# Graph stack on one Trainium2 core: z of four batches turned by VectorE, five more rows through DRAM, row columns stored element by element

## The chip, the core and the metric

One core of one Trainium2 chip runs the whole program. It has five engines that run beside each other: TensorE (PE in the profile, with PEld for its weight loads), VectorE (DVE), ScalarE (ACT), GpSimd (POOL) and the queue engine SyncE (SP), which here only issues DMAs. The metric is the device time of one execution in microseconds; lower is better. The time before is the median of three runs.

## The reference

Four layers run one after the other on `x` of 16 batches x 1024 nodes x 256 features, all in float32, with one weighted adjacency `adj` (1024 x 1024, some 1.6% of it set, the diagonal included):

```python
# layer 0: edge scores, a masked sum, a plain sum
S   = sigmoid(relu(h@W1[:d] [u] + h@W1[d:] [v] + b1) @ W2 + b2)   # one per edge u, v
z   = beta1*h + beta2*((S*A).T @ h @ Wa + ba) + beta3*((A.T @ h)*h @ Wm + bm)
# layer 1
z   = z + relu(A @ z @ W.T + b)
# layers 2 and 3: attention over all nodes, with adj as a bias, each with its own weights
feats  = z @ W1.T
f1     = feats @ W2 + b2
coefs  = softmax(leaky_relu(f1[:, None] + f1[None, :]) + adj)
z      = coefs @ feats + bias2 + z
```

The change lies in layers 2 and 3 only. Layer 3's result, node by feature, is the output.

## The kernel before, in words

**Tiling.** A node tile is 128 nodes (`P`), so a batch has eight (`NT`); a half is 512 nodes (`HN`, two of them, `NV`, four tiles each, `HT`). Between layers z is kept feature-major: `z[i]` is 128 partitions x 2 feature halves (`DH`) x 1024 nodes. The 16 batches go in four groups of four (`GB`, `NGR`).

**The main stream.** After the score-free work of all batches, each group runs `with_edges` (the masked sum of layer 0), `layer_one` for two batches at a time, and then layers 2 and 3 of its batches. Groups 0 to 2 do this in `group_layers`, in the order layer 2 of batches 0 to 3, layer 3 of batches 0 to 3. The last group runs as two pairs in `pair_layers`. A layer of a batch is made of:

- `front`: eight node tiles, each two products with the weights, giving `f` (feats and, in column D, f1 without its constant). PE writes a bank, ACT copies it out (L1392).
- the scale of the softmax: the code needs f1 of all nodes along a row in every partition (`r`), and the largest of them. It has two ways. `scales` (when `row` is None) turns the eight columns of f and the column of maxima by nine PE transposes. `to_row` (when a DRAM row is given) turns one 128 x 9 column tile by a PE transpose, copies it out by ACT, stores it in DRAM with a queue of SP (L1415) and loads it back twice, spread over all partitions (`rho`, L1416, and `tops`, L1417); `from_row`, some ticks later, takes the maximum on DVE (L1422) and goes on with a Relu on ACT (L1424). Both end in `scaled`.
- `sums`: twice (v = 0, 1) eight steps jt; in each DVE builds a tile m of 128 x 512 (L1475) and PE multiplies it with f into four banks. Three m tiles are built ahead (`AHEAD`).
- `second` or `third`: the end of a half. `second` turns the result back to feature-major and adds it to z. `third` makes the output: it needs z node-major, so `early` adds the bias to z on ACT (L1896) and turns two node tiles at a time by PE into a bank at the steps jt = 6 and 7 (L1905); `finish` adds that bank on DVE (L1921) and stores to `out` from ACT's queue.

**Order.** `later` is a list of work with a count of ticks. `tick` is called in `front` (two times), in `sums` (at every even jt) and in `projected` of layer one; what falls due is written at that place. `front` of the next batch is written ahead of `sums` of the current one, so a row made by `to_row` has the whole of the current `sums` before it is used; that of a group's first front has the second `layer_one`. A side stream of edge scores for the next group (gathers and scatters by POOL, products on DVE, sums on ACT) is woven in by `side.along`, and in the last group a stream that gathers layer one's messages by lists (`with_lists`). The framework then orders each engine's instructions by its own estimate of times, so the order on an engine is not exactly the written one; `paced` holds an instruction behind a recent product.

**Buffers that the change touches.** Eight PSUM banks; `gd_pool` (four tiles for edge scores, in the last pair for `msg`); `zs` with tag `u` (two tiles of the side stream's sources); `row_d`, a DRAM row per layer and batch.

Of the kernel before, what the change touches and what calls it, by code (L numbers as in the profile page):

```python
# [81 lines left out]
def gnn_stack_kernel(  # L82
# [41 lines left out]
    def bank():  # L124
        return psum[-1].tile([P, HN], F32, tag="bank", name="bank")
# [70 lines left out]
    R = 1 + D  # L196
# [92 lines left out]
    NGR = B // GB  # L289
# [636 lines left out]
    with tc.If(listed > 0) as arm:  # L926
        with ExitStack() as stack:
# [452 lines left out]
            def front(x, weights, row=None):  # L1380

                doing[0] = "fronts"
                wT = weights.wT
                f = ttile("feats").rearrange("p (t d) -> p t d", t=NT)
                for jt in range(NT):
                    ps = bank()
                    for dh in range(DH):
                        product(
                            ps[:, : D + 1], x[:, dh, jt * P : (jt + 1) * P], wT[:, dh, :],
                            start=dh == 0, stop=dh == DH - 1,  # L1390
                        )
                    nc.scalar.activation(f[:, jt, :], ps[:, : D + 1], AF.Copy)  # L1392
                    if jt % 4 == 1:
                        tick()
                    yield 0.86
                made = {}
                if row is None:
                    top = small.tile([P, 1], F32, tag="top", name="top")
                    nc.vector.tensor_reduce(top, f[:, :, D], AX.X, ALU.max)
                    later.append([1, lambda: scales(f, weights, made, top)])  # L1400
                else:
                    column = small.tile([P, NT + 1], F32, tag="column", name="column")
                    nc.vector.tensor_copy(column[:, :NT], f[:, :, D])
                    nc.vector.tensor_reduce(column[:, NT:], f[:, :, D], AX.X, ALU.max)
                    later.append([2, lambda: to_row(f, weights, made, row, column)])
                return made

            def to_row(f, weights, made, row, column):

                r = two.tile([P, N], F32, tag="rho", name="rho")  # L1410
                tops = two.tile([P, P], F32, tag="tops", name="tops")
                ps = bank()
                nc.tensor.transpose(ps[: NT + 1, :P], column, ident)
                nc.scalar.activation(r[: NT + 1, :P], ps[: NT + 1, :P], AF.Copy)
                nc.sync.dma_start(row.rearrange("(t p) -> t p", p=P), r[: NT + 1, :P])  # L1415
                nc.sync.dma_start(r, bcast_rows(row[:N], N))  # L1416
                nc.sync.dma_start(tops, bcast_rows(row[N:], P))  # L1417
                later.append([4, lambda: from_row(f, weights, made, r, tops)])
# [42 lines left out]
            def sums(made, v, finish, early=None):  # L1461

                doing[0] = "sums"
                while "f" not in made:
                    tick()
                f, r, ta = made["f"], made["r"], made["ta"]
                ms = made.setdefault("m", [])
                steps = made.setdefault("steps", [(w, jt) for w in range(NV) for jt in range(NT)])
                acc = [bank() for _ in range(HT)]
                for jt in range(NT):  # L1470
                    while steps and len(ms) < AHEAD:
                        w, kt = steps.pop(0)
# [12 lines left out]
                    if jt % 2 == 0:  # L1485
                        tick()
                    if early:
                        early(v, jt)
                    yield 1.7
                finish(v, acc)  # L1490
                yield 1.2

            def with_adj(main):

# [392 lines left out]
                return finish  # L1887


            def third(z, i, b):  # L1890
                turned_back = []

                def early(v, jt):
                    if v == 0 and jt == 2:
                        for dh in range(DH):
                            nc.scalar.activation(  # L1896
                                z[i][:, dh, :], z[i][:, dh, :], AF.Identity, bias=gat3.bias2[:, dh : dh + 1]
                            )
                    if jt < NT - 2:
                        return  # L1900
                    ps = bank()
                    for k in range(2):
                        it = v * HT + (jt - NT + 2) * 2 + k
                        for dh in range(DH):
                            nc.tensor.transpose(  # L1905
                                ps[:, k * D + dh * P : k * D + (dh + 1) * P],
                                z[i][:, dh, it * P : (it + 1) * P], ident,
                            )
                    turned_back.append(ps)

                def finish(v, acc):
                    for c in range(0, HT, 2):
                        ps = turned_back.pop(0)
                        it = v * HT + c
                        st = four.tile([P, 2, D + 1], F32, tag="st", name="st")
                        share = small.tile([P, 2], F32, tag="share", name="share")
# [9 lines left out]
                        later.append([1, functools.partial(nc.scalar.dma_start, to, st[:, :, :D])])  # L1926
                return finish, early

            def pair_layers(b, z, first):

                yield from first

                m0 = yield from front(z[0], gat2)
                m1 = yield from front(z[1], gat2)
                yield from sums(m0, 0, second(z, 0))
                yield from sums(m0, 1, second(z, 0))
                yield from sums(m1, 0, second(z, 1))
                m0 = yield from front(z[0], gat3)
                yield from sums(m1, 1, second(z, 1))
                t0, t1 = third(z, 0, b), third(z, 1, b)  # L1940
                yield from sums(m0, 0, *t0)
                m1 = yield from front(z[1], gat3)
                yield from sums(m0, 1, *t0)
                yield from sums(m1, 0, *t1)
                yield from sums(m1, 1, *t1)
                catch_up()

            def group_layers(g, z):
# [1 line left out]

                made = {}

                def fronts(layer, i, row=True):
                    row = row_d[layer, g * GB + i] if row else None
                    made[layer, i] = yield from front(z[i], (gat2, gat3)[layer], row)

                def next_hw(hw, k):
                    hw.append(load_hw((g + 1) * GB + k))
# [6 lines left out]
                def spread(loads):  # L1965

                    for k, load in enumerate(loads):
                        later.append([1 + 3 * k // 2, load])

                order = [(layer, i) for layer in range(2) for i in range(GB)]  # L1970
                beside = (lambda main: main) if g else with_adj
                yield from beside(layer_one(z[:2]))
                yield from fronts(0, 0, row=False)
                yield from beside(layer_one(z[2:]))
                assert not to_load and not to_exp
                for n, (layer, i) in enumerate(order):
                    if n + 1 < len(order):
                        yield from fronts(*order[n + 1])
                    if n == 2 * GB - 2:
                        hw, nz = [], load_z(g + 1)  # L1980
                        spread([functools.partial(next_hw, hw, k) for k in range(GB - 1)] + [next_z] * 2)
                    if n == 2 * GB - 1:
                        spread([functools.partial(next_hw, hw, GB - 1), next_z])
                    ends = third(z, i, g * GB) if layer else (second(z, i),)
                    yield from sums(made[layer, i], 0, *ends)
                    if n == 2 * GB - 1:
                        soon(g + 1)
                    yield from sums(made[layer, i], 1, *ends)
# [32 lines left out]
            for g in range(NGR):  # L2021
# [6 lines left out]
                else:  # L2028
# [2 lines left out]
                    with_lists(itertools.chain(  # L2031
                        first_pair, pair_layers(g * GB, z[:2], layer_one(z[:2], wide_quarters))
                    ))
                    for _ in pair_layers(g * GB + 2, z[2:], from_lists(z[2:], msg)):
                        pass
            assert next(side.steps, "end") == "end"
            psum.pop()
# [130 lines left out]
```

## Time and profile before

| what | us |
|---|---|
| median of three runs | 2999.75 (2998.23 to 3000.82) |
| the profiled execution's own time | 2996.18 |
| its span, first to last instruction | 2994.5 |
| PE busy | 2969.8 |
| PEld, DVE, ACT, POOL busy | 2139.4, 2107.0, 1828.2, 1711.4 |
| granted TensorE clock | 1.000 throughout |

The layers' sums run in these stretches, by the time of L1403 and L1399 in the trace: group 0 from 1082 to 1431 us, group 1 from 1613, group 2 from 2141 to 2489, the first pair from 2690, the second from 2845 to the end. A line of the profile's list of groups gives a line of the kernel, engine, operation, output and inputs, shape and count; behind the first bar the busy time of the group and the mean duration of one in ns; behind the second the idle time of the engine just before, and what ended it. A line of the timeline gives the start and the length in us, engine, line, operation and count. SPq means the queue instructions of SP.

### The profile page before, as it was taken

The numbers are of one execution on the slowest core, as the hardware profiler recorded it, in microseconds if no ns is written. First come the engines' busy times: TensorE is split into PE (matmuls) and PEld (weight loads), VectorE is DVE, ScalarE is ACT, GpSimd is POOL, SyncE is SP. The second block draws the span as 40 slices with busy tenths as digits, with TensorE's granted clock in tenths as the row PEclk, the third lists the DMA queues.
The fourth block names the chain that finished last, engine by engine and source line by source line (L and its number), as shares of the span: only waits on it lengthen the run. The fifth ranks groups of instructions, "written<-read, shape, count | busy, mean of one in ns | idle before, by whom it ended". The sixth has DMA issues, their size and how long they took to land. (4 is left out here: it accounts for less than half of the span.)

```text
span 2994.5 us, 41906 instructions
## 1 busy us (share of the span) xinstructions
PE 2969.8 (99%) x11750; PEld 2139.4 (71%) x11750; DVE 2107.0 (70%) x4173; ACT 1828.2 (61%) x6522; POOL 1711.4 (57%) x1501
## 2 busy tenths in 40 slices
PE   8999999999999999999999999999999999999999
PEld 5545555555548757888875788888568888858888
DVE  8877666666775677888666888876678843388744
ACT  3436665666766776787776678777767833213342
POOL 1136576677664757766667767667677520277500
PEclk9999999999999999999999999999999999999999
DMA  8899999989999986668988766899876546586600
GB/s 292 316 385 313 317 320 285 299 239 276 272 313 349 313 301 193 173 191 293 329 285 268 218 181 186 283 348 292 272 208 176 158 143 210 170 295 180 168 1 30
DMA packets 323467, 736.78 MB, mean 246 GB/s; under 512 B 51533, under 2 KB 145802, under 8 KB 318106
## 3 DMA queue, kind: packets, MB, share of 16 engines
q0 software_dynamic: 129664, 394.14, 44.1%
q1 hardware_dynamic: 152170, 268.05, 26.6%
q10 hardware_dynamic: 41392, 71.84, 6.4%
q8 instruction: 95, 1.56, 0.2%
q14 instruction: 146, 1.20, 0.1%
HBM read 597.34 MB, written 136.53 MB: 245 GB/s over the span
## 5 line engine op out<-in xcount | busy, mean ns | idle before, releaser
L1034 ACT ACTIVATE z<-z 128x257 f32<-128x257 f32 x2432 | 984.3, 410 | 455.8 <-DVE z L1068 272.5
L143 PE MATMUL bank<-feats,m 128*128 128x257 f32 x4096 | 908.3, 380 | 3.3 <-DVE m L1475 2.2
L143 PEld LDWEIGHTS bank<-feats,m 128*128 128x128 f32 x4096 | 769.7, 190 | 112.9 <-DVE m L1475 2.6
L946 POOL DMA_INDIRECT z<-v_d,slot_v x512 | 596.2, 1164 | 379.7 <-ACT z L1034 180.4
L951 POOL DMA_INDIRECT dense_d<-gt,slot_at x512 | 578.1, 1129 | 212.5 <-PE bank L143 117.9
L1066 DVE TENSOR_TENSOR z<-z,u 128x580 f32<-128x580 f32 x608 | 462.1, 760 | 323.4 <-PE bank L143 254.0
L1034 ACT ACTIVATION_READ_ACCUMULATOR z<-z 128x1 f32 x2432 | 467.4, 192 | 0.0
L1475 DVE SCALAR_TENSOR_TENSOR m<-rho,tau,adj_sb 128x512 f32<-128x512 f32 x512 | 377.1, 747 | 111.7 <-PE bank L143 104.2
L143 PE MATMUL bank<-gc,hw 128*128 128x256 f32 x1920 | 416.8, 379 | 2.9 <-ACT gc L1517 2.3
L143 PEld LDWEIGHTS bank<-gc,hw 128*128 128x128 f32 x1920 | 363.9, 190 | 55.1 <-ACT gc L1517 4.3
L1067 DVE TENSOR_TENSOR z<-z,u 128x448 f32<-128x448 f32 x608 | 376.9, 620 | 0.0
L143 PE MATMUL bank<-w1p,hT 128*128 128x385 f32 x1024 | 340.6, 486 | 2.4 <-DVE sign L629 1.2
L143 PEld LDWEIGHTS bank<-w1p,hT 128*128 128x128 f32 x1024 | 192.9, 189 | 149.8 <-issue 19.9
L143 PE MATMUL bank<-g_wT,z 128*128 128x257 f32 x1024 | 230.4, 380 | 0.5 <-DVE z L1678 0.5
L143 PE MATMUL bank<-adj_sb,h 128*128 128x512 f32 x504 | 223.3, 592 | 0.8 <-ACT stage L257 0.8
L143 PEld LDWEIGHTS bank<-g_wT,z 128*128 128x128 f32 x1024 | 192.0, 190 | 31.1 <-issue 2.4
L374 ACT ACTIVATE st<-bank 128x385 f32<-128x385 f32 x256 | 122.9, 485 | 140.4 <-PE bank L143 108.1
L946 POOL DMA_INDIRECT z<-v_d,x_node x96 | 124.2, 1293 | 119.5 <-PE bank L143 55.3
L143 PEld LDWEIGHTS bank<-adj_sb,h 128*128 128x128 f32 x504 | 95.5, 190 | 115.6 <-issue 106.5
L1068 DVE TENSOR_TENSOR z<-z,sign 128x128 f32<-128x128 f32 x608 | 173.7, 286 | 0.0
L1517 ACT ACTIVATE gc<-gd 128x512 f32<-128x512 f32 x112 | 126.4, 1138 | 74.7 <-PE bank L143 47.3
L143 PE MATMUL bank<-adjT_in,t 128*128 128x512 f32 x336 | 147.6, 592 | 0.0
(257 smaller groups left out, 3327.1 us busy)
## 6 DMA issues: line engine op xcount, KB each, us to landing
gd<-dense_d SPq DMA_DIRECT2D x128, 512.0 KB
dense_d<-zero ACTq DMA_DIRECT2D x64, 512.0 KB
h<-in_x_dram SPq DMA_DIRECT2D x19, 1024.0 KB
adjT_in<-sumT_d SPq DMA_DIRECT2D x70, 256.0 KB
u_d<-st SPq DMA_DIRECT2D x128, 128.5 KB
v_d<-st SPq DMA_DIRECT2D x128, 128.5 KB
u<-u_d POOLq DMA_DIRECT2D x32, 514.0 KB
hw_d<-st SPq DMA_DIRECT2D x128, 128.0 KB
```

The source lines that it names most:

```text
L143: recent.append(nc.tensor.matmul(*args, **kw))
L374: nc.scalar.activation(st[:, cols], ps[:, :half], AF.Copy)
L946: return paced(nc.gpsimd.indirect_dma_start(out=dst, out_offset=None, in_=src[:], in_offset=bass.IndirectOffsetOnAxis(ap=at, axis=0), **how,))
L951: return paced(nc.gpsimd.indirect_dma_start(out=dst[:], out_offset=bass.IndirectOffsetOnAxis(ap=at, axis=0), in_=src, in_offset=None,))
L1034: nc.scalar.activation(zk[:, c, :], zk[:, c, :], AF.Copy, accum_out=s[:, k, c : c + 1])
L1066: paced(nc.vector.tensor_tensor(big, big, uk[:, :, :BIG], ALU.max))
L1067: paced(nc.vector.tensor_tensor(low, low, uk[:, :, BIG:], ALU.min))
L1068: nc.vector.tensor_tensor(mixed, mixed, sign[:, None, :].to_broadcast([P, GB, MIXED]), ALU.mult)
L1475: nc.vector.scalar_tensor_tensor(m, r[:, cols], ta[:, kt : kt + 1], ea[:, kt, cols], ALU.max, ALU.mult)
L1517: paced(nc.scalar.activation(t, scores, AF.Copy), 16 - 2 * i)
```

## The change

Three edits.

1. In group 2 (layer 3 of batches 2 and 3) and in the last pair (layer 3 of both), z is turned to node-major by DVE instead of PE. Right behind the `front` that reads z, ACT adds the bias, and 32 DVE transposes of 32 x 32 blocks are listed in `to_turn`, each over 32 partitions x 256 elements. `sums` takes two from the list at every step jt, so they lie beside the sixteen steps ahead of the batch's own layer 3. The result goes to borrowed SBUF tiles (`gd` tiles, for batch 3 of group 2 two `u` tiles); `early` does nothing for these batches and `finish` reads the tiles.
2. Five more fronts take the way over DRAM: the first front of groups 0 to 2, and layer 2 of the second batch of both pairs.
3. `to_row` stores the column tile (128 partitions x 9) directly, element by element, without PE and ACT, and it falls due one tick earlier.

```diff
@@ front
-                    later.append([2, lambda: to_row(f, weights, made, row, column)])
+                    later.append([1, lambda: to_row(f, weights, made, row, column)])
@@ to_row
-                ps = bank()
-                nc.tensor.transpose(ps[: NT + 1, :P], column, ident)
-                nc.scalar.activation(r[: NT + 1, :P], ps[: NT + 1, :P], AF.Copy)
-                nc.sync.dma_start(row.rearrange("(t p) -> t p", p=P), r[: NT + 1, :P])
+                nc.sync.dma_start(row.rearrange("(t p) -> p t", p=P), column)
@@ sums
                     if early:
                         early(v, jt)
+                    for _ in range(2):
+                        if to_turn:
+                            to_turn.pop(0)()
                     yield 1.7
...
+            to_turn = []
@@
+            def turned_by_vector(x, room):
+                for dh in range(DH):
+                    nc.scalar.activation(x[:, dh, :], x[:, dh, :], AF.Identity, bias=gat3.bias2[:, dh : dh + 1])
+                Q = 32
+                for v in range(NV):
+                    cols = slice(v * HN, (v + 1) * HN)
+                    src = x[:, :, cols].rearrange("p h (t c q) -> p h t c q", c=P // Q, q=Q)
+                    dst = room[v].rearrange("p (t h a r) -> p h t a r", h=DH, a=P // Q, r=Q)
+                    for a in range(P // Q):
+                        for c in range(P // Q):
+                            to_turn.append(functools.partial(
+                                nc.vector.transpose, out=dst[c * Q : (c + 1) * Q, :, :, a, :],
+                                in_=src[a * Q : (a + 1) * Q, :, :, c, :],
+                            ))
+                return room
@@ third
-            def third(z, i, b):
+            def third(z, i, b, nodes=None):
                 def early(v, jt):
+                    if nodes is not None:
+                        return
...
-                        ps = turned_back.pop(0)
+                        if nodes is None:
+                            ps = turned_back.pop(0)
+                        else:
+                            ps = nodes[v][:, c * D : (c + 2) * D]
@@ pair_layers
-                m1 = yield from front(z[1], gat2)
+                m1 = yield from front(z[1], gat2, row_d[0, b + 1])
...
                 m0 = yield from front(z[0], gat3)
+                n0 = turned_by_vector(z[0], gd_room()) if by_vector else None
                 yield from sums(m1, 1, second(z, 1))
-                t0, t1 = third(z, 0, b), third(z, 1, b)
+                t0 = third(z, 0, b, n0)
                 yield from sums(m0, 0, *t0)
                 m1 = yield from front(z[1], gat3)
+                n1 = turned_by_vector(z[1], gd_room()) if by_vector else None
+                t1 = third(z, 1, b, n1)
@@ group_layers
-                yield from fronts(0, 0, row=False)
+                yield from fronts(0, 0)
...
                         yield from fronts(*order[n + 1])
+                        if order[n + 1][0] and g == NGR - 2 and order[n + 1][1] > 1:
+                            at = order[n + 1][1]
+                            nodes[at] = turned_by_vector(z[at], gd_room() if at < GB - 1 else [
+                                zs.tile([P, GB * R], F32, tag="u", name="zn")[:, : HT * D] for _ in range(NV)
+                            ])
...
-                    ends = third(z, i, g * GB) if layer else (second(z, i),)
+                    ends = third(z, i, g * GB, nodes.get(i)) if layer else (second(z, i),)
@@ the last group
-                    for _ in pair_layers(g * GB + 2, z[2:], from_lists(z[2:], msg)):
+                    for _ in pair_layers(g * GB + 2, z[2:], from_lists(z[2:], msg), True):
```

More of the change, by code (lines that the diff above doesn't have):

```diff
@@ L1887, in second, with gd_room @@
                 return finish
-            def third(z, i, b):
+            def turned_by_vector(x, room):
[13 more added lines that the diff above has]
+                return room
+            def gd_room():
+                return [
+                    gd_pool.tile([P, QN, GB], F32, tag="gd", name="zn").rearrange("p a b -> p (a b)") for _ in range(NV)
+                ]
+            def third(z, i, b, nodes=None):
                 turned_back = []
                 def early(v, jt):
+                    if nodes is not None:
+                        return
                     if v == 0 and jt == 2:
@@ L1927, in third, with pair_layers @@
                 return finish, early
-            def pair_layers(b, z, first):
+            def pair_layers(b, z, first, by_vector=False):
                 yield from first
                 m0 = yield from front(z[0], gat2)
-                m1 = yield from front(z[1], gat2)
+                m1 = yield from front(z[1], gat2, row_d[0, b + 1])
                 yield from sums(m0, 0, second(z, 0))
@@ L1951, in group_layers, with fronts @@
                 made = {}
-                def fronts(layer, i, row=True):
-                    row = row_d[layer, g * GB + i] if row else None
-                    made[layer, i] = yield from front(z[i], (gat2, gat3)[layer], row)
+                def fronts(layer, i):
+                    made[layer, i] = yield from front(z[i], (gat2, gat3)[layer], row_d[layer, g * GB + i])
                 def next_hw(hw, k):
@@ L1968, in spread @@
                         later.append([1 + 3 * k // 2, load])
+                nodes = {}
                 order = [(layer, i) for layer in range(2) for i in range(GB)]
```

## The prediction

> **What bounds the kernel now.** I read the page first, then busy time by stage, then the TensorE groups by shape, then the timeline around each operation that the change touches.
>
> ```profile
> PE 2969.8 (99%) x11750; PEld 2139.4 (71%) x11750; DVE 2107.0 (70%) x4173; ACT 1828.2 (61%) x6522; POOL 1711.4 (57%) x1501
> 2300.00:2400.00 100.00, 100.00 (x488) 87.49 (x487) 80.73 (x177) 83.30 (x313) 59.27 (x48) 1.00 0.53 149
> 2400.00:2500.00 100.00, 100.00 (x488) 87.56 (x487) 44.82 (x91) 33.14 (x66) 18.47 (x16) 1.00 0.53 172
> ```
>
> The second and third lines give PE, PEld, DVE, ACT and POOL busy in 100 us, then clock and DMA share. PE has no free time; its waits sum to 18.5 us, half of it in the first 25 us. So PE work that goes is time that goes, unless a new wait takes its place. Busy time overstates a matmul, so the price of one comes from start distances:
>
> ```profile
> L1905 PE MATMUL bank<-ident,z 128*128 128x128 f32 x256 | 38.4, 273 | 0.0
> L1438 PE MATMUL bank<-ident,feats 128*128 128x128 f32 x88 | 11.4, 273 | 0.0
> L1413 PE MATMUL bank<-ident,column 128*9 128x128 f32 x21 | 5.7, 273 | 0.0
> L1443 PE MATMUL bank<-ident,top 128*128 128x128 f32 x11 | 3.2, 291 | 0.4 <-DVE top L1399 0.3
> ```
>
> ```profile
> 2435.46 0.27 PE L1413 MATMUL bank<-ident,column 128*9 128x128 f32 x1
> 2435.57 7.10 PE L143 MATMUL bank<-feats,m 128*128 128x257 f32 x32
> 2442.51 0.60 PE L1905 MATMUL bank<-ident,z 128*128 128x128 f32 x4
> 2442.95 1.90 PE L143 MATMUL bank<-feats,m 128*128 128x257 f32 x8
> ```
>
> One row transpose holds the next matmul back by 2435.57 - 2435.46 = 0.11 us; four z transposes by 0.44, 0.11 each. The nine of `scales` run from 1614.14 to the next matmul at 1615.12: 0.98.
>
> **What goes from PE.** z: 4 batches x 16 transposes x 0.11 = 7.0 us. Row columns: 21 x 0.11 = 2.3. Five fronts leave `scales` for a row: 5 x 0.98 = 4.9. Sum 14.2 us, spread over 130 instructions. By busy time it would be 9.6 + 5.7 + 11.4 x 40/88 + 3.2 x 5/11 = 21.9, the upper end. I take 14.2, since start distance is what a saturated engine gives back.
>
> **What VectorE gets.** 128 transposes of 32 partitions x 256 elements; none is in the trace. Nearest rows:
>
> ```profile
> 7.75 0.41 DVE L588 TENSOR_SCALAR to_own<-places,place,scale 128x256 f32<-128x256 f32 x1
> 8.07 0.42 DVE L588 TENSOR_SCALAR to_other<-places,place,back 128x256 f32<-128x256 f32 x1
> L1921 DVE SCALAR_TENSOR_TENSOR st<-st,share,bank 128x256 f32<-128x256 f32 x128 | 55.5, 477 | 2.1
> ```
>
> From 0.32 (start to start) to 0.48 us; I take 0.42, what L588 lasts without the overlap. A batch costs 32 x 0.42 = 13.4 us. It lies beside 16 steps of `sums`, about 29.5 us of PE. There DVE now has (PE, PEld, DVE, ACT, POOL, clock, DMA):
>
> ```profile
> 2390.00:2400.00 10.00, 10.00 (x48) 8.67 (x47) 5.92 (x13) 9.89 (x41) 0.00 (x0) 1.00 0.08 27
> 2430.00:2440.00 10.00, 10.00 (x48) 8.66 (x48) 4.00 (x7) 2.72 (x4) 0.00 (x0) 1.00 0.17 53
> ```
>
> From 2390 to 2420 it is 5.92 + 5.05 + 5.54 = 16.5 of 30, from 2430 to 2460 14.5; in the last pair sixteen m of about 0.72 and two finishes of 2, 15.5. With 13.4 more that is 27.9 to 29.9 of 29.5: nearly full, not over. Three m tiles (1.74 us of PE each) are built ahead and the next front needs no m for 7 us. I price this at 1 us in all; at 0.48 a batch is 15.4 and the excess about 2 us a batch, most of it within those m. The page "VectorE: DVE Perf Modes", section on two Vector instructions with no wait between them, has an instruction held until earlier ones end when its starting quadrant changes. By that the overlap of 0.08 is lost on nearly all 128, 10 us of DVE that the stretches above still take.
>
> The z biases (L1896, 1.15 us x 2 a batch) only move, to behind the front; ACT is 27% busy there at 2430: nothing, and if ACT were full, 2.3 us a batch. `third` reads z from SBUF where it read PSUM, same shape: nothing; four PE banks less are held. Where buffers are borrowed: two gd tiles for batch 2 are read out by about 2462, and SP asks for the next gd at 2471.78, so nothing waits.
>
> **The rows.** The store goes from nine runs of 512 B to 1,152 elements of 4 B, without the ACT copy (21 x 0.26 us, not on the path), and its column no longer waits for PE. Now:
>
> ```profile
> 2431.47 0.17 DVE L1403 COPY column<-feats 128x8 f32<-128x8 f32 x1 [6.21 <-ACT feats L1392]
> 2436.06 0.29 SPq L1415 DMA_DIRECT2D row_d<-rho  x1
> 2437.32 0.32 SPq L1416 DMA_DIRECT2D rho<-row_d  x1
> 2448.36 0.29 DVE L1422 TENSOR_REDUCE shift<-tops 128x1 f32<-128x128 f32 x1 [0.55 <-PE bank L143]
> ```
>
> The store lands 1.26 us after its issue here, 5.5 at worst. Issuing 1,152 elements should hold SP about 1 us (w2c's 256 take 0.45, nine runs 0.29); only the row's own loads stand directly behind. Landing, by the nearest rows:
>
> ```profile
> 0.82 0.45 SPq L186 DMA_DIRECT2D w2c<-in_L_gnn_W_dram  x1
> 4.05 0.17 DVE L552 TENSOR_SCALAR above<-w2c 128x2 f32<-128x2 f32 x1 [3.09 <-DMA w2c<-in_L_gnn_W_dram]
> ...
> 335.38 0.37 SPq L1016 DMA_DIRECT2D got<-extra_d  x1
> 346.70 0.41 DVE L1021 COPY x_a<-got 128x24 f32<-128x24 f32 x1 [4.52 <-DMA got<-extra_d]
> ```
>
> 256 single elements took 3.2 us: less 1.3 fixed, 1.9 x 1152/256 + 1.3 = 10 us. 768 runs of 64 B took 11.3 in a crowded stretch (DMA share 0.96): 10 x 1.5 + 1.3 = 16.3. Lower end 1.3. I take 10, the row of the same kind. The two loads behind need at most 5.0 (tops issued 1234.91, reduce 1239.89, no DMA wait). So 15 at most from column to reduce. What covers it: column to reduce is now 14.2 to 18.2 us, median 16.7; the chain starts and the reduce is emitted one tick earlier, 3.5 us, leaving 13.2; then DVE may stand about 4 us on ready m tiles: 17.2. Covered in the median; in the tightest row 14.7 against 15. Behind the waiting reduce on DVE stand m products and score work, behind the Relu on ACT score sums and evacuations; PE waits for the m.
>
> "DMA: Bandwidth & Descriptors", Rules for kernel authors, says a non-contiguous last dimension becomes one descriptor per element and should be rearranged; "VectorE: DVE Perf Modes", The three transpose paths, calls a strided copy 19 times slower than the crossbar path. As an estimate, 19 x the present mean of 2.7 us is 51 us, 39 beyond the cover, some 1,000 us over 26 rows. The w2c row shows nothing of that size.
>
> Fronts (0,0) of three groups are different: their chain runs inside layer one. At 1613.3 the column is ready while SP's 1 MB load of 1607.94 still fills the DMA (share 0.94 up to 1620, then 0.03), so the row lands by about 1629 and its broadcasts by 1634. ACT then has 6 us of scaling and three y copies behind it, DVE the feature sums; PE needs the last y near 1640, since eight banks let it finish the projection. Zero to 3 us each; I take 1 in all.
>
> **Sum.** The profiled execution took 2996.18, span 2994.5. 2996.18 - 14.2 + 1 + 1 = 2984.0; the median of the runs lies 3.57 above that execution, so 2987.5.
>
> **Rivals.**
> 1. *Rows too late* (slower). If the store needs over 12 us, DVE stops with m unready. For it: the got row's 16.3 and DMA shares of 0.61 to 0.76 in the sums of groups 0 and 1. Against: group 2 and the pairs are lighter, and w2c. At 15 us it costs some 3 us on 14 rows, 42 - 14 = 28 over: about 3028; it turns the sign from some 13 us. Chance 0.14.
> 2. *VectorE becomes the bound* in the four batches. At 0.6 us a transpose a batch is 19 us on 16, 35 of 29.5, less about 3 ahead: 3 us x 4 = 12, and 2997 to 2998. For: odd access shapes; against: every 256-element row is under 0.48. Chance 0.10, within 0.2%.
> 3. *The gain is taken elsewhere.* Groups 1 and 2 open with a stage at 0.96 to 0.98 DMA share, and the list stream ends at 2834.5 where PE already waits 0.5 us; 3.5 + 1 us could stay there, and a new order on the engines may cost what it does at 1415 to 1420 now, 3.2 us. 14.2 - 2 - 8 = 4, near 2995. Chance 0.08, within 0.2%.
> 4. *Main case*, 2978 (busy-time end, 21.9) to 2993. Chance 0.68.
>
> A measurement of this kernel tells 0.2% (6 us) from nothing. Faster 0.68, same 0.18, slower 0.14. The range takes the main case and rivals 2 and 3 with the first of the late rows: 2978 to 3001.
>
> **What would show it.** PE with 130 fewer instructions, about 2955 busy and still 99%; no L1413 group; L1905 at 192; 128 DVE transposes of 0.4 us beside sums; L1422 and L1424 with no DMA wait; L1416 some 10 us behind L1415. DVE waits of several us on tops, or PE waits on DVE m above 10 us, would make it wrong.

## The result

| | before | after |
|---|---|---|
| median (lowest to highest, 4 runs each) | 2998.99 (2996.52 to 3000.82) | 3163.9 (3160.84 to 3165.92) |
| span of the profiled execution | 2994.5 | 3159.1 |
| mean granted TensorE clock | 1.000 | 0.979 |

The changed kernel is slower: 1.055 times the time before, interval 1.0537 to 1.0562. Forecast were 2987.5 us and a range of 2978 to 3001.

The page of the changed kernel, busy time and DMA:

```profile
PE 3010.2 (95%) x11620; PEld 2154.7 (68%) x11620; DVE 2153.9 (68%) x4306; ACT 1822.8 (58%) x6496; POOL 1696.3 (54%) x1501
DMA packets 354897, 739.74 MB, mean 234 GB/s; under 512 B 81872, under 2 KB 176592, under 8 KB 349536
```

PE has its 130 instructions fewer, and yet 40.4 us more of busy time. The span grew by 164.6 us: PE's idle time by 124.2 (3159.1 - 3010.2 = 148.9, from 24.7), its busy time by 40.4. As some 14 us of work were taken out, some 54 us of the busy time must be the same matmuls taking longer: the largest group, bank<-feats,m, has a mean of 391 ns where it had 380. Of the DMA packets, 31,430 are new; 26 rows of 1,152 elements are 29,952, and e1 below, with edits 1 and 2 but nine runs, has 324,998 packets, 29,899 fewer than here. That agrees with the rule of one descriptor per element in the Trainium skill ("DMA: Bandwidth & Descriptors", Rules for kernel authors).

The waits of the changed kernel (engine, what it waited to do, releaser: total us, times, longest):

```profile
DVE shift L1419 <- DMA tops<-row_d: 185.5, 25, 15.5
ACT rho L1421 <- DVE shift L1420: 159.9, 21, 16.0
PE bank L143 <- DVE m L1472: 90.2, 31, 8.2
PE bank L1880 <- ACT val L1873: 11.7, 3, 6.2
SPq L1413 <- DMA row_d<-column: 306.5, 26, 18.8
```

Before, L1422 (now L1419) never waited for DRAM. Now VectorE stops at 25 of the 26 rows, 7.4 us each. One of them, on the timelines of VectorE, SyncE, TensorE and ScalarE, in group 2:

```profile
2425.50 0.22 DVE L1404 TENSOR_REDUCE column<-feats 128x1 f32<-128x8 f32 x1
2425.76 0.37 SPq L1412 DMA_DIRECT2D row_d<-column  x1
2436.17 0.32 SPq L1413 DMA_DIRECT2D rho<-row_d  x1
2436.54 0.73 SPq L1414 DMA_DIRECT2D tops<-row_d  x1
2445.37 0.28 DVE L1419 TENSOR_REDUCE shift<-tops 128x1 f32<-128x128 f32 x1 [7.03 <-DMA tops<-row_d]
...
2424.53 19.25 PE L143 MATMUL bank<-feats,m 128*128 128x257 f32 x88
2446.97 0.44 PE L1880 MATMUL bank<-ident,val 128*128 128x128 f32 x2 [2.54 <-ACT val L1873]
2448.04 10.63 PE L143 MATMUL bank<-feats,m 128*128 128x257 f32 x40 [0.63 <-DVE m L1472]
...
2446.44 0.48 ACT L1873 ACTIVATE val<-bank,share 128x256 f32<-128x256 f32 x1 [7.41 <-DVE share L1867]
```

Read it so: the store goes out at 2425.76 and its loads 10.4 us later; VectorE comes to the reduction at 2438.34 and stands until 2445.37. A reciprocal (share, L1867) is queued behind it; ScalarE waits 7.41 us for that, and TensorE, which has used up the m tiles built ahead, 2.54 for ScalarE's val and 0.63 for the next m. This row shows the rarer case: over the whole run TensorE waited 31 times for m (90.2 us) and 3 times for this val (11.7 us). Then come 40 matmuls in 10.63 us, 266 ns each, where the 88 ahead took 219: a stop is followed by slower matmuls. The granted clock in steps of 4 us shows why, and then two stages (columns as in the prediction):

```profile
2444.00:2448.00 4.00, 0.87 (x6) 0.40 (x4) 2.63 (x10) 1.56 (x3) 3.30 (x3) 1.00 0.52 205
2448.00:2452.00 4.00, 3.96 (x11) 3.17 (x12) 4.00 (x8) 4.00 (x12) 2.60 (x2) 0.57 0.48 132
2452.00:2456.00 4.00, 4.00 (x20) 3.51 (x19) 3.31 (x6) 3.68 (x17) 1.34 (x2) 1.00 0.00 0
...
1200.00:1300.00 100.00, 87.00 (x400) 75.10 (x399) 66.31 (x145) 63.02 (x244) 58.08 (x50) 0.95 0.61 132
2400.00:2500.00 100.00, 87.59 (x382) 74.70 (x383) 71.03 (x156) 69.90 (x260) 51.27 (x45) 0.90 0.59 137
```

Behind the stop PE runs 4 us at a clock of 0.57, 11 matmuls where 20 fit. The same 4 us in steps of 1 us:

```profile
2448.00:2449.00 1.00, 0.96 (x3) 0.85 (x4) 1.00 (x2) 1.00 (x3) 0.69 (x2) 0.69 0.36 33
2449.00:2450.00 1.00, 1.00 (x3) 0.76 (x3) 1.00 (x4) 1.00 (x6) 1.00 (x1) 0.50 0.70 160
2450.00:2451.00 1.00, 1.00 (x4) 0.78 (x3) 1.00 (x3) 1.00 (x4) 0.90 (x1) 0.50 0.82 333
2451.00:2452.00 1.00, 1.00 (x5) 0.79 (x4) 1.00 (x3) 1.00 (x4) 0.00 (x0) 0.61 0.04 2
```

In the two stages PE is busy 87% where it was 100%, and the mean clock is 0.95 and 0.90 (it was 1.00).

### The profile page after: what moved, and what is told of

The parts are those of the page before. It is cut to its first block, busy times and chain, and to the rows that moved or that the text cites. A ratio compares the mean times of both kernels' runs of the same rounds, so it can differ in the third digit from the quotient of the medians.

```text
span 3159.1 us, 41758 instructions
## 1 busy us (share of the span) xinstructions
PE 3010.2 (95%) x11620; PEld 2154.7 (68%) x11620; DVE 2153.9 (68%) x4306; ACT 1822.8 (58%) x6496; POOL 1696.3 (54%) x1501
## 5 line engine op out<-in xcount | busy, mean ns | idle before, releaser
L143 PE MATMUL bank<-feats,m 128*128 128x257 f32 x4096 | 946.4, 391 | 93.2 <-DVE m L1472 90.2
L143 PEld LDWEIGHTS bank<-feats,m 128*128 128x128 f32 x4096 | 795.1, 196 | 224.0 <-DVE m L1472 100.9
L951 POOL DMA_INDIRECT dense_d<-gt,slot_at x512 | 570.1, 1114 | 244.3 <-PE bank L143 122.9
L1066 DVE TENSOR_TENSOR z<-z,u 128x580 f32<-128x580 f32 x608 | 460.9, 758 | 325.4 <-PE bank L143 217.3
```

Source lines behind the costliest of these rows:

```text
L143: recent.append(nc.tensor.matmul(*args, **kw))
L951: return paced(nc.gpsimd.indirect_dma_start(out=dst[:], out_offset=bass.IndirectOffsetOnAxis(ap=at, axis=0), in_=src, in_offset=None,))
L1066: paced(nc.vector.tensor_tensor(big, big, uk[:, :, :BIG], ALU.max))
```

## The experiments

The change has three edits: the turn of z on VectorE in four batches (edit 1), five more fronts through DRAM (edit 2) and the store by element (edit 3). Some of the runs were on one of two chips on which the kernel before takes 3037 us (marked *: e1 to e4 on the one, e14 to e17 on the other), the rest on chips on which it takes 2997 to 3000; each ratio is to runs of the kernel before on the same chip, and idle times are compared between runs of like chips only.

**Which edit.** Three runs take the change apart.

```
e1: the changed kernel, with edit 3 undone (transpose, eviction, nine runs)
e2: the kernel before, with edit 3 alone (to_row one tick earlier too; the store in short):
-   ps = bank(); transpose; activation(Copy); dma_start(row "(t p) -> t p", r[:9, :P])
+   nc.sync.dma_start(row.rearrange("(t p) -> p t", p=P), column)
e3: the kernel before, with edit 1 alone
```

> Edits 1 and 2 stay, edit 3 is undone: PE turns the column again, nine runs of 512 B are stored, one tick later. Theory A (the element store makes the rows late: DVE waited 185.5 us for tops in 25 of 26 rows, PE then idled and its granted clock fell to 0.979): DVE waits for tops below 15 us in all, clock 1.000, 2986 to 2992 us. Rival B (the DVE transposes or the borrowed tiles cost): still above 3050. Rival C (the five new rows cost, above all the three inside layer one, where DVE waited 13 to 16 us each): those waits stay near 10 us, time 3000 to 3030.

> The kernel before with edit 3 alone: 21 rows stored as 1,152 elements, one tick earlier. Theory A: the 21 rows in sums waited 135 us of the 185.5, so 21 waits of about 6 us on tops, PE idle and slow clock in that share of the loss: 3100 to 3140 us. Rivals B and C: 2995 to 3000.

> The kernel before with edit 1 alone: z of four batches turned by 128 DVE transposes. By the prediction's own term, 64 x 0.11 = 7.0 us go from PE and about 1 us comes back: 2992 to 2994 us, clock 1.000, a transpose 0.35 to 0.48 us. Rival B: above 3020, with PE waits on DVE m in the last pair.

Measured*: e1 1.0014 (1.0001 to 1.0028), e2 1.0529 (1.0503 to 1.0555), e3 1.001 (0.9995 to 1.0024). Edit 3 alone is nearly the whole loss, on the 21 rows that the kernel before had, and more than theory A gave it (3100 to 3140 of 2999 us, 1.034 to 1.047). In the waits of e2:

```profile
DVE shift L1419 <- DMA tops<-row_d: 133.4, 18, 11.4
PE bank L143 <- DVE m L1472: 106.1, 34, 9.8
```

Without it, the other two edits showed no gain on that chip; more on this below.

**Are 5 us right for the two loads?** e4 is the kernel before with its nine runs, but the reduction stands two ticks behind the store instead of four, so that the loads' landing shows as a wait.

```
-   later.append([4, lambda: from_row(...)])
+   later.append([2, lambda: from_row(...)])
```

> The kernel before (nine runs, PE transposes), only the reduce is written two ticks after the store instead of four, some 7 us earlier, so that the landing of the two loads shows as a DVE wait. If the loads take at most 5.0 us also there, as the prediction had it from two rows, column to reduce of 9.7 us is short by 4.6 + 2.7 + 5 - 9.7 = 2.6 us at most, and the waits sum to under 50 us. If the loads take the 8 us that they took behind the element store, the waits are 5 to 6 us each, 110 us in all, and the loads were never as short as the prediction took them.

Its wait at the reduction:

```profile
DVE shift L1422 <- DMA tops<-row_d: 47.2, 16, 7.0
```

Measured*: one run of 3109.57 us, 2.4% above the median of before. From the issue of tops to the reduction it took 5.3 us on the mean of the 16 rows that waited, 3.6 to 9.7: the prediction's 5.0 was near. In the changed kernel the same stretch took 7.6 (25 rows, 3.9 to 10.3). So behind a store by element the loads, too, took longer. In the row of the changed kernel shown above the core's DMA moved 12 to 41 GB/s from 2428 to 2438 us, and then 269 to 407 until 2446, at a share of 0.93 to 1.05: the loads landed among other traffic. That this is why they took longer is not shown. And 47 us of waits on VectorE came with a loss of 72 us; as this run also moves the reduction in VectorE's order, it does not show how much of that the waits cost.

**Take the wait away, keep the elements.** e5 is the changed kernel with `later.append([7, ...])` for the reduction.

> The changed kernel, with the elements stored as there, but the reduction of tops comes seven ticks behind the store and not four: some 22 us instead of 12.6, against a store and two loads that took 12.7 and 7.6 us, 20.3 in all. Theory (the rows come too late for the reduction): VectorE's wait for tops falls from 185 us to below 40, TensorE's idle time from 149 to below 75, and the time to 0.997 to 1.010 of before; what is left is m tiles made some 10 us later. Rival 1 (the 30,000 small writes slow the core's other traffic and its engines whenever they run): the wait goes, the time stays at 1.03 or more. Rival 2 (the m tiles can't be 10 us later, as the sums of the front before end by then): VectorE's wait goes, and as much comes as TensorE's wait for VectorE's m, over 100 us, the time again above 1.04.

Measured: 1.031 (1.0292 to 1.0328). The store's loads went out 12.5 us behind it as before; of the wait 43.8 us are left, 42.0 of them at the three fronts (0,0), but 94 us of idle time stay on PE, 72 more than in the kernel before (e0 below). The waits of e5:

```profile
DVE shift L1419 <- DMA tops<-row_d: 43.8, 5, 16.0
PE bank L143 <- DVE m L1472: 30.5, 18, 4.3
```

Taking VectorE's stop away gave back 2.4 of the 5.5%. The time misses the theory (up to 1.010) and meets rival 1 (1.03 or more) just so; rival 2's sign, over 100 us of waits for m, did not come. Of TensorE's idle time 13.7 us lie at the fronts (0,0). VectorE also waits 72.2 us for the gathered z that L1066 reads (`slot_v`), where e0 has 11.8; what slows them is not shown.

**A landing with fewer pieces.** e6 (all three edits) and e8 (edit 3's place alone, in the kernel before) store the column as 128 runs of 32 bytes and let the row lie by partitions in DRAM; only that row comes back, the maximum is taken of all of it, and m reads r with a stride.

```
+   nc.sync.dma_start(row[:N].rearrange("(p t) -> p t", p=P), column)
+   m <- max(r viewed as (n t) -> t n, ta) * ea        (in words)
```

> The kernel before, unchanged, for a profile on the chip of the experiments, where it takes 3037 us instead of 2999. If the 1.4% between the two chips are TensorE's, its busy time here is the 2969.8 us of the first profile or a little more and the rest is idle: about 2976 busy and 58 idle, in the stages where the batches of eight rows end. Then the vector-only run (2980.7 busy, 54 idle) and the run with the old store (2976.6 busy, 59 idle) had 14 us of work fewer and lost them again to waits. If instead the busy time here is about 2990 with 45 idle, TensorE is slower on this chip and the 14 us did come off the busy time, and went into idle time.

> The changed kernel, but the row lies in DRAM by partitions: the column goes out as 128 runs of 32 bytes, only the row of 1,024 comes back, the maximum is taken of it (128x1024 where tops was 128x128), and m reads it with a stride of 32 bytes. Still no transpose and no eviction on the way. If landing time goes with the number of pieces (9 runs 3.1 us from issue to the next issue, 1,152 elements 12.7), 128 runs land in about 4.2 us, and one load behind them in 5 to 6, inside the 12.6 us of cover: no wait for DRAM is left, and the time is 0.995 to 1.002 of before. If a store of less than 64 bytes a run is slow for its smallness, not for the count, it lands in 8 us or more and the loss is still above 1.01. The strided read may cost m: its mean of some 0.6 to 0.7 us would show it, 16 tiles by 26 fronts; 0.1 us more each would be 42 us of VectorE.

> The kernel before with that other store alone: nine runs of 512 bytes, a transpose and an eviction are replaced by 128 runs of 32 bytes for the same 21 rows; the four batches' z are turned on TensorE and five fronts keep their own way. TensorE has 21 transposes fewer (2.3 us) and ScalarE 21 evictions. If the landing is hidden, 0.997 to 1.001 of before. Compared with the run that also has the other two edits it says what those two are worth together: by the prediction 11 us (0.4%), by the two runs so far about nothing.

e0 came out on one of the faster chips, the one of e5, e6 and e8: 2996.45 us, PE busy 2972.9, idle 21.9. e6: 1.0349 (1.0331 to 1.0367), e8: 1.0201 (1.0184 to 1.0218). The store itself did what was expected: loads 3.5 and 3.2 us behind it (nine runs in e0: 2.8), and no more than three rows with a wait. Most of the loss is another one, in e8's groups by shape:

```profile
L1469 DVE SCALAR_TENSOR_TENSOR m<-rho,tau,adj_sb 128x512 f32<-128x512 f32 x512 | 502.9, 1004 | 73.2 <-PE bank L143 66.9 <-ACT rho L1448 6.2
```

m takes 1004 ns where e0 has 745, 126 us more of VectorE; the maximum, over 1,024 values instead of 128, takes 19 more. TensorE waits 36.9 us for m, where e0 has 1.3. Reading one operand 32 bytes apart made these runs useless as a cure; as a measurement of the landing they stand.

**Do the elements harm when nobody waits for them?** e11 is the kernel before, with one more store by element per row, to a place that nobody reads. e16 issues it from ScalarE's queue. e14 holds it behind the reduction (its values are the column plus the reduced maximum).

```
e11 +  nc.sync.dma_start(idle.rearrange("(t p) -> p t", p=P), column)
e16 +  nc.scalar.dma_start(idle.rearrange("(t p) -> p t", p=P), column)
e14 +  nc.vector.tensor_scalar(behind, column, sh[:, 0:1], None, ALU.add)
    +  nc.sync.dma_start(idle.rearrange("(t p) -> p t", p=P), behind)
```

> The kernel before, with one more store for each of its 21 rows: the column by element, 1,152 of 4 bytes, to a place that nobody reads, issued by SyncE behind the two loads. Nothing waits for it. Theory (the loss is the row's lateness alone): 0.999 to 1.004 of before. Rival (the small writes slow what runs beside them, whoever waits): the loads of the row take 7.6 us instead of 5.2, the gathers and VectorE's adds wait for DRAM more, and the time is 1.01 or more.

> The kernel before with the idle element store once more, now held back: the values stored are the column plus the reduced maximum, so that the store can only go out behind the reduction (in the run with idle elements the trace shows it 5 us ahead of the row's own store, which then landed in 10.8 us, so lateness was in it after all). One tensor_scalar of 9 elements more a row on VectorE. Theory (the loss is the row's lateness alone): the row's store lands in 3 to 4 us, its loads in 5 to 6 behind the cover, no wait for tops, 0.999 to 1.004 of before. Rival (the small writes slow what runs beside them): waits for gathers and for dense_d grow, the time is 1.01 or more.

> The run with idle elements ahead of the row's own store, but ScalarE issues them, on its own queue. If elements delay only what stands behind them on their queue, the row's store lands in 3 to 4 us again, VectorE waits under 15 us for tops in all, and the time is 0.999 to 1.006 of before. If they hold up the engines that move the data, whatever the queue, the row's store lands in 8 us or more, and the time is 1.02 to 1.035 again.

Measured: e11 1.0319 (1.03 to 1.0338), e14* 1.0061 (1.0035 to 1.0087), e16* 1.0246 (1.0217 to 1.0275). In e11 the idle store was not behind the loads, where the expectation has it: its column is ready first, and it went out ahead of the row's own nine runs. A row each of e11, e16 and e14 (ACTq means the queue instructions of ACT):

```profile
2325.19 0.37 SPq L1419 DMA_DIRECT2D idle_d<-column  x1
2328.49 0.29 SPq L1416 DMA_DIRECT2D row_d<-rho  x1
2339.59 0.32 SPq L1417 DMA_DIRECT2D rho<-row_d  x1
```

```profile
2377.12 0.37 ACTq L1419 DMA_DIRECT2D idle_d<-column  x1
2380.24 0.29 SPq L1416 DMA_DIRECT2D row_d<-rho  x1
2391.10 0.32 SPq L1417 DMA_DIRECT2D rho<-row_d  x1
```

```profile
2368.20 0.29 SPq L1416 DMA_DIRECT2D row_d<-rho  x1
2370.73 0.32 SPq L1417 DMA_DIRECT2D rho<-row_d  x1
2382.24 0.37 SPq L1428 DMA_DIRECT2D idle_d<-behind  x1
```

With an element store under way, nine runs of 512 bytes take 11 us to land instead of 2.5, on the same queue (e11, mean 10.4) and on another one (e16, mean 9.2) alike. So what is held up is not the queue that issued the elements but something that both queues share. e14 has the same elements with nothing behind them that is waited for: 0.6%, between the theory's 0.4 and the rival's 1.0. VectorE waits 82.8 us for tops in e11, 58.5 in e16 and 1.6 in e14. Most of the loss of e11 and e16 is therefore lateness of the row, and a small part the traffic itself.

**Lateness without elements.** e15 and e17 have edits 1 and 2 and nine runs; in e15 the row's steps come two ticks later, with the reduction where e5 has it; e17 begins one tick behind the column, as the changed kernel does.

```
e15: later.append([4, lambda: to_row(...)])    # was 2
e17: later.append([1, lambda: to_row(...)])    # was 2
```

> The version with both other edits and the store in nine runs, but everything of the row two ticks later: the reduction eight ticks behind the column, where the changed kernel with a later reduction had it too, and no element store at all. Theory (a row that is late makes m late, whatever store it comes from): VectorE has no wait for tops and TensorE waits for m, 1.015 to 1.03 of before, as there (1.031). Rival (it is the element stores): 0.998 to 1.003.

> The version with both other edits and the store in nine runs, but begun one tick behind the column and reduced at five, as in the changed kernel, which then differs from it only in the store. If the place of the reduction in VectorE's order costs something by itself (reduced at four ticks, the kernel before lost 2.4%, with 47 us of waits for tops), it is 1.005 to 1.015; if only the landing counts, the row lands in 8 to 9 us within a cover of 12 to 13, and the time is 0.997 to 1.002.

Measured*: e15 1.0146 (1.0122 to 1.0169), at the low end of the theory's range, and e17 1.013 (1.0097 to 1.0163), beside e1's 1.0014 on the other slower chip. In e15 VectorE waits 9.5 us for tops and TensorE 9.4 for m, but 16.8 for ScalarE's val: a row that is later by its place alone costs 1.3%. Of e5's 3.1% that leaves more than half: the traffic (0.6% by e14) and the 13.7 us at the fronts (0,0) (0.5%) bring it to some 2.4, an estimate from runs on different chips, and the rest is open. e17 isn't the clean counterpart that it was meant to be: begun a tick earlier, its transposes stand on TensorE before the column is there (the waits of e17):

```profile
PE bank L1413 <- DVE column L1404: 12.2, 7, 4.2
DVE shift L1422 <- DMA tops<-row_d: 16.8, 4, 6.2
```

Its time lies in the range given for a cost of the reduction's place, but the 12.2 us are in it too, so the two aren't told apart.

**Does the landing go with the number of elements?** e10 splits the store in two, 512 elements after the fourth tile and 640 at the end. e18 and e19 store 576 and 288 elements, from 64 and 32 partitions; the rest of the row is filled by more loads of the same values, so e18 leaves half of the row and e19 three quarters of it out of the computation.

```
e10 +  nc.sync.dma_start(row[:HN].rearrange("(t p) -> p t", p=P), column[:, :HT])     # at jt == HT
    +  nc.sync.dma_start(row[HN:].rearrange("(t p) -> p t", p=P), column[:, HT:])     # at the end
e18 +  nc.sync.dma_start(row[: 9 * 64].rearrange("(t p) -> p t", p=64), column[:64])  # and two loads of r
e19 +  nc.sync.dma_start(row[: 9 * 32].rearrange("(t p) -> p t", p=32), column[:32])  # and four loads of r
```

> The changed kernel, but the column goes out in two stores by element: the 512 of the first four tiles when their eviction is done, some 7 us ahead of the rest, and 640 with the maxima at the end; the reduction stays four ticks behind the second. If the landing goes with the number of elements (9 pieces 3.1 us, 128 pieces 3.4, 1,152 elements 12.7), 640 land some 3 + 0.56 x 9.6 = 8.3 us after issue, 4.4 earlier than all of them, and VectorE's wait for tops, 7.4 us a row on the mean, falls to about 3: 185 us to 60 to 90, the ratio from 1.055 to 1.02 to 1.03. If the number of elements under way is what counts and not the last store's, or if an element store has one fixed price, the landing is still 12 us or more and the ratio stays at 1.045 to 1.06.

> The changed kernel with half of the element store: only partitions 0 to 63 go out, 576 elements of 4 bytes; the row's 1,024 places are filled by two loads of the same 512, and the maximum is taken over 64 partitions, so half of the row is left out of the computation. All else, the reduction's place too, is as in the changed kernel. If the landing grows with the number of elements (3.2 us for nine pieces, 12.7 for 1,152), the loads go out 8 us behind the store, VectorE's wait for tops falls from 185 to 60 us or less, and the time is 1.01 to 1.025 of before. If an element store has a price by itself, it lands in 11 us or more and the time stays above 1.04.

> The same with a quarter: partitions 0 to 31, 288 elements, four loads of the same 256; three quarters of the row are left out of the computation. By the line through nine and 1,152 pieces the loads go out 5.5 us behind the store, VectorE hardly waits for tops (below 25 us), and the time is 0.998 to 1.012 of before, against 0.998 without any element store. If element stores disturb beyond their landing it stays above 1.015.

Measured: e10 1.0906 (1.0879 to 1.0932), e18 1.051 (1.0486 to 1.0533), e19 1.0538 (1.0517 to 1.0559). All three expectations of the theory missed, and e10 is beyond its rival's range too. A row's stores and first load on SyncE's queue:

```profile
2489.53 0.37 SPq L1389 DMA_DIRECT2D row_d<-column  x1
2493.43 0.37 SPq L1415 DMA_DIRECT2D row_d<-column  x1
2509.24 0.33 SPq L1416 DMA_DIRECT2D rho<-row_d  x1
```

This is e10, the stores at 2489.53 and 2493.43: its first part left only 3.9 us ahead of the second, and the two took 19.7 us together where one whole store took 12.3. In e18 and e19 the loads go out 10.4 and 8.0 us behind the store. From the pieces of one store to its landing that gives: 9 of 512 bytes 2.8 us, 128 of 32 bytes 3.2 to 3.5, 288 of 4 bytes 8.0, 576 10.4, 1,152 12.3. It grows with the elements, but no line through the nine pieces fits. As the further loads took longer in their turn, the reduction came 19.5 and 20.4 us behind the store on the rows that waited, and 20.3 in the changed kernel: three kernels with a quarter, a half and all of the elements, the same arrival, and a loss of 5.1 to 5.5%. Why 288 elements need 8 us, and whether that is the width of four bytes or the partitions that they come from, is open.

**The better kernel.** e12 is the kernel before with edit 2 alone, e13 is e1 once more, both on a chip on which before takes 3000 us.

> The kernel before, and five more fronts put their rows through DRAM, in nine runs of 512 bytes with the transpose and the eviction; nothing else. By the prediction TensorE loses five times nine transposes of 0.11 us and gains five: 4.4 us, and about 1 us comes back as a wait: 0.9985 to 1.000. If the first layer's rows, for which the sums start at once (they waited 13 to 16 us for tops in the changed kernel), cost TensorE a wait of 3 us or more each, the gain is gone: 1.000 to 1.004.

> The vector turns and the five rows, with the store in nine runs, once more, for its profile on the chip of the other runs of this call. TensorE's idle time was 59.5 us on a chip where the kernel before takes 3037 us; where before takes 2998 its idle time is 22. If the two edits bring new waits of their own (for VectorE's m and z beside the 128 transposes, for the first layer's rows), the idle time is 30 or more here too and the ratio 1.000 to 1.003; if the waits were that chip's, it is 22 to 26 and the ratio 0.996 to 0.998.

Measured: e12 0.9991 (0.9982 to 1.0), e13 0.9976 (0.9965 to 0.9986), that is 2992.62 us against 3000.01: on this chip a version that beats both kernels, by little. Its page's busy times, and two of its waits:

```profile
PE 2962.1 (99%) x11646; PEld 2129.6 (71%) x11646; DVE 2160.3 (72%) x4306; ACT 1829.0 (61%) x6522; POOL 1711.8 (57%) x1501
```

```profile
DVE shift L1422 <- DMA tops<-row_d: 14.6, 3, 6.0
PE bank L143 <- DVE m L1475: 7.5, 8, 3.8
```

Beside e0, PE is busy 10.8 us less (2972.9 to 2962.1) and idle 5.3 us more (21.9 to 27.2); the first profile of the kernel before has 2969.8 busy, so the 10.8 are good to some 3 us. The three waits for tops are those of the fronts (0,0). On the chip of e1 and e3 nothing of the gain was measured (1.0014 and 1.001); no profile of the kernel before was taken there, so what ate it is not known.

## Why the prediction was wrong

**The step that failed** is the landing of the row, "So 15 at most from column to reduce", held against a cover of "17.2: Covered in the median". It took 20.3 us from store to reduction on the rows that waited. Three terms of that sum, and one beside it:

- *The store*: 10 was taken from w2c's 256 elements in 3.2 us; it is 12.3 on the mean, 9.1 to 19.2. The row was near in kind and far in place: w2c goes out at 0.82 us with hardly anything beside it. In the middle of the sums 288 elements took 8.0 (e19). w2c is a load besides. The bound of 16.3 from the crowded got row held for 25 of the 26 rows. It stood in the text: with it the same sum is 21.3, over the cover, so the "at most" hung on the choice of 10.
- *The loads*: "at most 5.0" came from a row whose loads stood behind nine runs. Behind such a store 5.3 is right (e4), behind elements it is 7.6.
- *The cover*: 13.2 us was right, the changed kernel gave 12.85 on the rows that waited (13.8 without the three fronts (0,0)). The 4 us on top, "DVE may stand about 4 us on ready m tiles", weren't there to that extent: TensorE ran out of m, as the text feared, 31 times for 90.2 us in all. The example of 2438 shows a second way that the text doesn't name: VectorE also has the reciprocals, ScalarE's val stands on them, and TensorE on val (3 times, 11.7 us).
- *The fronts (0,0)*: "Zero to 3 us each; I take 1 in all." VectorE waited 15.5, 13.1 and 15.3 us there, and TensorE stood 19.5 us in all in front of layer one's next products:

```profile
1105.52 9.52 PE L143 MATMUL bank<-blocks,t 128*128 128x512 f32 x16 [5.52 <-DVE t L393]
1693.24 7.06 PE L143 MATMUL bank<-blocks,t 128*128 128x512 f32 x11 [4.80 <-DVE t L393]
2283.26 2.04 PE L143 MATMUL bank<-blocks,t 128*128 128x512 f32 x2 [9.19 <-issue]
```

The third has no releaser that the profile names. With nine runs (e13) VectorE waited 4.1 to 6.0 us at these fronts, and TensorE did not stop at these products.

**Rival 1 was the case that came**, and its price was too small. Its sum of store and loads at 15 + 5 us is what was measured, but "some 3 us on 14 rows" became a stop of 7.4 us on 25 rows. It took group 2 and the pairs for lighter: that was so for the pairs' two rows (2.5 and 3.8 us), but group 2 waited like the others, as at 2425.76, in a stage with a DMA share of 0.59. And it counted lost time one for one: PE idles 124 us more, and some 54 go to the lower clock, of which the prediction has nothing.

**What held.** The 128 transposes last 435 ns (forecast 0.42). Ten in a row took 4.62 us, as the timeline of the changed kernel has it:

```profile
2561.49 4.62 DVE L1488 STREAM_TRANSPOSE zn<-z 32x256 f32<-32x256 f32 x10
```

That is 0.46 from start to start, with none of the overlap that L588 has (0.32). It agrees with what the Trainium skill says on quadrants ("VectorE: DVE Perf Modes", Two Vector instructions with no wait between them). The price of `third` from SBUF was right, 481 ns against 475. Edits 1 and 2 with nine runs were to bring 14.2 - 2.3 - 5 x 0.11 - 2 = 9.4 us; e13 has 7.4 (4.2 to 10.5), with 10.8 off the busy time and 5.3 more idle. VectorE did not become the bound. SP's part was dearer on paper than on the chip: 1,152 elements are issued in 0.37 us, not 1. The estimate of 51 us a row took 19 times the landing of nine runs; the Trainium skill ("VectorE: DVE Perf Modes", The three transpose paths) has a DMA copy that transposes by strides 19 times slower than the crossbar's DMA transpose, which no run here has. Against nine runs it is 12.3 to 2.8 us, 4.4 times.

**By the prediction's own tests**, "DVE waits of several us on tops" and "PE waits on DVE m above 10 us" both came true.

## What to carry to other kernels

Price a transfer by the landing that it has in the stage where it runs, not by a row from the quiet start, and price the transfer behind it anew. When a wait is put on an in-order engine, list everything queued behind the waiting instruction and follow each to the bound engine; the cover ends at the first of them that is needed; here that was mostly m, sometimes val. A small edit that trades work on the bound engine (2.3 us here) for some 10 us of latency on a chain is a bad trade unless slack and latency are both known to a microsecond or two.

## What the runs showed of the hardware

- An element store delays another store that goes out while it is under way, whatever queue that is on: nine runs landed in 2.8 us without it, in 10.4 with it ahead on their queue, in 9.2 with it on another. With nothing urgent behind them, 21 such stores, with one small VectorE operation each, cost 0.6% (0.35 to 0.87).
- Where TensorE idles often, the loss is more than the idle time: stops of 2.54 and 0.63 us, with 0.44 of work between, were followed by a clock of 0.50 for about 3.4 us (worked out from the four steps of 1 us: (0.31 + 0.50 + 0.50 + 0.39) / 0.50). That length and that clock agree with the Trainium skill ("TensorE: Matmul & The Clock Gate", Part 1: The HAM clock gate), which has the clock halved behind an idle window of about 3.4 us until it has been busy for about as long. PE idle in the span and mean clock: 22 us and 0.999 (e0), 27 and 0.998 (e13), 94 and 0.991 (e5), 149 and 0.979 (the changed kernel), 236 and 0.966 (e10).
- A scalar_tensor_tensor of 128x512 with one f32 operand read 32 bytes apart took 1004 (e8) and 1065 ns (e6) instead of 745 (e0).
